# Splitting an expert's first and third weights into two buffers and two transfers, with a shorter Newton step for the norms

## The chip, the cores and the metric

The kernel runs on one core of a Trainium2 chip. The metric is the device time of one execution in microseconds. The time before is the median of three runs, 1347.77 us (1346.8 to 1350.46).

## The reference

The input is one sequence of 2048 rows of 512 numbers (float32). It is layer-normalised, and the normalised rows `xn` go two ways, whose results are added to the input:

```python
xn = layernorm(x)                       # (x - mean) / sqrt(var + 1e-5)
x + attention(xn) + ffn(xn)

# attention: 16 heads, two softmax maps each (d = 16), rotary, causal
f1, f2 = rfft(attn1, axis=time), rfft(attn2, axis=time)
f = (f1 - lambda_full * f2) * filt      # a Gaussian low-pass over time
a = irfft(f)
a = a * rsqrt(mean(a * a over the 32 of a head) + 1e-5) * rms_weight * (1 - LAMBDA_INIT)
a.reshape(T, 512) @ Wout

# ffn: 8 experts, each row goes to its best 2, and a shared expert for all rows
scores = softmax(xn @ gate_w.T); w, idx = top_k(scores, 2); w = w / sum(w)
y_e = (silu(xn @ w1[e]) * (xn @ w3[e])) @ w2[e]        # 512 -> 352 -> 512
shared = (silu(xn @ sw1) * (xn @ sw3)) @ sw2           # 512 -> 704 -> 512
```

## The kernel before

The kernel has three stages. The first normalises the rows in groups of 1, 1, 2, 4, 4 and 4 tiles of 128 rows, computes the routing, and makes rotated queries and keys, which it writes to device memory. The second, `middle`, is nine tenths of a millisecond of attention with the experts' products laid in between. The third, `ending`, does the filter over time as products with constant matrices, the norm over each head, the output product and the sum of all parts.

**Order.** In `middle` all five engines keep the order of the program text. The attention is a stream of units (one key block of one head, scores, exponential, mask, values, sums), four at a time. After each burst the loop calls `work()`, which takes the next step of the generator `experts()`. Each `yield` in that generator is one step with a weight in us, by which the loop paces the steps evenly over the stream. SyncE issues nearly all transfers, in program order: query and key loads (`qS`, `kS`) when a new attention chunk begins, the experts' weights, and the stores of the experts' rows to `ys`. Transfers share eight completion semaphores in turn, so an issue waits for the transfer eight before it.

**Experts.** Routed rows are sorted by expert into slots. A tile is 128 slots. Its steps are: `up_first`, four products `xh` with the first weights, tanh and a multiply; `up_third`, four products `xg` with the third weights and a multiply; the gather of later rows; the transpose of the next tile's rows (`xT`); and `down`, three products `xy` with the second weights, of the tile before. The first 26 tiles in `ORDER` belong to one expert each. The next six hold 64 slots of one expert and 64 of another, so that they need two sets of weights and each product is done in two halves. Two more one-expert tiles end the row. `sets[j]` says which weight sets tile `j` uses.

**Weights.** `wex` in device memory has one row of 4352 numbers per partition for each expert: first and third weights (2816, interleaved by 128-row block of the input dimension), then second weights (1536). Two more entries hold the shared expert. On chip there are two places, each with a buffer `wu` (1408 KB) and a buffer `wd` (768 KB). Set `n` uses place `n % 2`. `routed(j)` reads the expert's number on SyncE. `fetch_up` fills `wu` for set `n + 2` after `up_third` of the tile that used set `n`, since `wu` is free only then; `fetch_down` fills `wd` after `down`.

In the last block of the shared expert (steps `n` of `chunks`, in `experts`) the row order is loaded at `n == 0`, transposed at `n == 3`, and at `n == 5` the first rows are gathered and the first `fetch_up` is issued; the second follows after the block.

**Norms.** `rsqrt` and `newton` compute 1/sqrt with one Newton step: ScalarE takes the square root, VectorE the reciprocal and four more operations. VectorE adds the small constant to the variance before that (L360 in the first stage, L1237 in `means` of `Pair`, where it also divides by 32). There are six such steps in the first stage, and eight in the last, one for each pair of row tiles.

**The end.** `fetched` loads the input rows into `res`, adds the shared expert's rows, and then gathers each row's two expert rows from `ys` with adding transfers on GpSimd (L1136, L1138). `finished` and `last` add the output product on VectorE (L1289, L1300) and store.

Of the kernel before, what the change touches and what calls it, by code (L numbers as in the profile page):

```python
# [8 lines left out]
F32 = mybir.dt.float32  # L9
# [10 lines left out]
P = 128  # L20
# [30 lines left out]
WUP = NE * 2 * FI  # L51
# [18 lines left out]
def block_kernel(  # L70
# [39 lines left out]
    neglam = cpool.tile([P, 1], F32, name="neglam")  # L110
    ones = cpool.tile([P, P], F32, name="ones")
# [12 lines left out]
    def rsqrt(pool, dst, src, n):  # L124

        root = pool.tile([P, n], F32, tag="rs_root", name="rs_root")
        nc.scalar.activation(root, src, AF.Sqrt)
        newton(pool, dst, src, root, n)

    def newton(pool, dst, src, root, n):  # L130
        y = pool.tile([P, n], F32, tag="rs_y", name="rs_y")
        nc.vector.reciprocal(y, root)
        z = pool.tile([P, n], F32, tag="rs_z", name="rs_z")
        nc.vector.tensor_mul(z, src, y)
        nc.vector.tensor_mul(z, z, y)
        nc.vector.tensor_scalar(z, z, -0.5, 1.5, ALU.mult, ALU.add)
        nc.vector.tensor_mul(dst, y, z)
# [5 lines left out]
    w_sb = [  # L143
        (wp.tile([P, WUP], F32, name=f"wu{i}"), wp.tile([P, WCOL - WUP], F32, name=f"wd{i}")) for i in range(2)
    ]

    def fetch_up(e, i, eng):
        eng.dma_start(w_sb[i][0], e[:, :, :WUP].rearrange("o p w -> p (o w)"))

    def fetch_down(e, i, eng):  # L150
        eng.dma_start(w_sb[i][1], e[:, :, WUP:].rearrange("o p w -> p (o w)"))

# [4 lines left out]
    def expert(mp, fps, yp=None, stores=2, by_scalar=False):  # L157
# [19 lines left out]
        def up_half(ws, xT, i, name):  # L177
            dst = bank([P, FI], name)
            for c in range(NE):
                o = (2 * c + i) * FI  # L180
                for r, w in parts_of(ws):
                    nc.tensor.matmul(  # L182
                        dst[r, :], xT[:, c, r], w[:, o : o + FI], start=(c == 0), stop=(c == NE - 1),
                        skip_group_check=True,
                    )
            return dst

        def up_first(w, xT):

            h = up_half(w, xT, 0, "xh")  # L190
            s = mp.tile([P, FI], F32, tag="s", name="xtanh")
            nc.scalar.activation(s, h, AF.Tanh, scale=0.5)
            nc.vector.scalar_tensor_tensor(s, s, 1.0, h, ALU.add, ALU.mult)
            return s

        def up_third(w, xT, s):

            g = up_half(w, xT, 1, "xg")
            nc.vector.tensor_mul(s, g, s)
            return s  # L200

        def up(w, xT):
            return up_third(w, xT, up_first(w, xT))
# [31 lines left out]
        return up_first, up_third, up, turned_back, (down, down_products, stored), transposed  # L235

    def shared_expert(mp, fps, places=SCH):
# [4 lines left out]
        def hidden(k, x, dst=None):  # L242

            if dst is None:
                dst = fps.tile([P, x.shape[2]], F32, tag="f", name="wh")
            for c in range(NE):
                o = (NE * k + c) * P
                nc.tensor.matmul(  # L248
                    dst, w_sb[o // WUP][0][:, o % WUP : o % WUP + P], x[:, c, :], start=(c == 0), stop=(c == NE - 1)
                )  # L250
            return dst
# [29 lines left out]
        def result(us, t, which=range(SCH), y=None):  # L281

            if y is None:
                y = fps.tile([P, E], F32, tag="f", name="wy")
            for i in which:
                nc.tensor.matmul(  # L286
                    y, us[i][:, t * P : (t + 1) * P], w_sb[i // NF][1][:, i % NF * E : (i % NF + 1) * E],
                    start=(i == 0), stop=(i == SCH - 1),
                )
            return y  # L290
# [4 lines left out]
    with ExitStack() as pools:  # L295
# [38 lines left out]
        for i in range(2):  # L334
            fetch_up(wex[NX + i : NX + i + 1], i, nc.sync)
            fetch_down(wex[NX + i : NX + i + 1], i, nc.sync)
# [21 lines left out]
        def normalised(done, many, mv):  # L358
            var = lp.tile([P, many], F32, tag="var", name="var")
            nc.vector.tensor_scalar(var, mv[:, :, 1], EPS, None, ALU.add)  # L360
            rstd = lp.tile([P, many], F32, tag="rstd", name="rstd")
            rsqrt(lp, rstd, var, many)
# [158 lines left out]
        _, _, _, _, (_, _, stored), _ = expert(ep, eps, stores=EARLY)  # L521
# [76 lines left out]
    def middle(general):  # L598


        with ExitStack() as pools:
# [29 lines left out]
            def experts():  # L631
# [5 lines left out]
                _, _, _, _, (_, _, stored), _ = expert(sp, fps, mp, by_scalar=True)  # L637
                _, _, _, chunks, result = shared_expert(sp, fps)
                for t0 in range(EARLY, NT - 1, TQ):
# [3 lines left out]
                    for n, us in enumerate(chunks(xnT[:, :, cols], u_last)):  # L643
# [7 lines left out]
                        elif last and n == 3:  # L651
                            ps = bank([P, 2, NR], "ps_w")
# [4 lines left out]
                        elif last and n == 5:  # L657


                            xr = [rows_of(j) for j in ORDER[:2]]  # L660
                            es = [routed(2 * ORDER[0])]
                            fetch_up(es[0], 0, nc.sync)
                        yield 3.45 * (t1 - t0) / TQ
                    if last:
                        es.append(routed(2 * ORDER[1]))
                        fetch_up(es[1], 1, nc.sync)
# [7 lines left out]
                up_first, up_third, _, turned_back, (down, _, _), transposed = expert(rp, fps, mp, by_scalar=True)  # L674
                for i in range(2):
                    fetch_down(es[i], i, nc.sync)
# [12 lines left out]
                def tile_down(j, uT):  # L689
                    tj = ORDER[j]  # L690
                    return places(j, 1), uT, ys[tj * P : (tj + 1) * P, :], wcol[:, tj : tj + 1]

                for j in range(NR):
# [3 lines left out]
                    yield 2.9 if late else 2.4  # L697
                    u = up_third(places(j, 0), xT, half)
                    if j + 2 < NR:
                        xr.append(rows_of(ORDER[j + 2]))  # L700
                    for n in sets[j]:
# [3 lines left out]
                        fetch_up(es[n + 2], n % 2, nc.sync)  # L705
# [3 lines left out]
                    if late:  # L709
                        down(*late)  # L710
                        for n in sets[j - 1]:
                            fetch_down(es[n + 2], n % 2, nc.sync)
# [7 lines left out]
                fetch_down(wex[NX : NX + 1], 0, nc.sync)  # L720
# [381 lines left out]
    def ending():  # L1102
# [3 lines left out]
        with tc.tile_pool(name="tail1", bufs=1) as t1, tc.tile_pool(name="tail2", bufs=2) as t2, tc.tile_pool(  # L1106
# [9 lines left out]
            _, _, _, _, (_, _, stored), _ = expert(tp, fps, by_scalar=True)  # L1116
            hidden, gated, times, _, result = shared_expert(t2, fps, 2)
            fetch_down(wex[NX + 1 : NX + 2], 1, nc.scalar)
# [106 lines left out]
            class Pair:  # L1225
# [8 lines left out]
                def means(self):  # L1234
                    self.ms = tp.tile([P, 32], F32, tag="ms", name="ms")
                    nc.vector.tensor_reduce(self.ms, self.sq.rearrange("p i (h d) -> p (i h) d", d=32), AX.X, ALU.add)
                    nc.vector.tensor_scalar(self.ms, self.ms, 1.0 / 32, EPS, ALU.mult, ALU.add)  # L1237

                    self.root = tp.tile([P, 32], F32, tag="root", name="root")
                    nc.scalar.activation(self.root, self.ms, AF.Sqrt)  # L1240

                def scales(self):

                    r = tp.tile([P, 32], F32, tag="rms", name="rms")
                    newton(tp, r, self.ms, self.root, 32)
# [103 lines left out]
    with tc.If(nc.values_load(more[0:1, 0:1], min_val=0, max_val=1) > 0):  # L1349

        with tc.tile_pool(name="before_more", bufs=1) as gap, tc.tile_pool(name="more", bufs=2) as mp, tc.tile_pool(
# [3 lines left out]
            _, _, up, turned_back, (down, _, _), transposed = expert(mp, fps)  # L1355
            for j in range(NR, NS):
# [14 lines left out]
                u = up([w[:, :WUP] for w in ws], transposed(x))  # L1371
                down([w[:, WUP:] for w in ws], turned_back(u), ys[j * P : (j + 1) * P, :], pairs[:, 1:])
# [50 lines left out]
def _experts(w1, w3, w2, sw1, sw3, sw2):  # L1423
# [5 lines left out]
    for e in range(NX):  # L1429
        up = a[e, :, :WUP].reshape(P, NE, 2, FI)  # L1430
        for i, w in enumerate((w1[e], w3[e])):
            up[:, :, i] = w.reshape(NE, P, FI).transpose(1, 0, 2)
# [51 lines left out]
```

## Time and profile before

| | |
|---|---|
| time, median of three runs | 1347.77 us |
| the profiled execution's own time, and its span | 1349.09 us, 1347.3 us |
| granted TensorE clock, mean of the span | 0.994 |
| moved by DMA | 215.06 MB, mean 160 GB/s |
| weight loads `wu`, on SyncE | 44 of 1408 KB |
| weight loads `wd`, on SyncE | 44 of 768 KB (one more on ScalarE) |
| first stage and shared rows, to the first scores | 0 to about 254 us |
| attention with the shared expert's products | about 254 to 600 us |
| attention with one-expert tiles | about 600 to 1070 us |
| attention with two-expert tiles | about 1070 to 1197 us |
| last two tiles, then the third stage | about 1197 us to the end |

How to read the profile: the page gives each engine's busy time and share of the span, and in forty slices the busy tenths and the clock that TensorE was granted. A timeline row gives start, duration, engine, line of the kernel, operation, result and operands, how many instructions were merged into the row, and in brackets the idle time before it with what ended it. `PE` is TensorE, `DVE` VectorE, `ACT` ScalarE, `POOL` GpSimd, and `SPq` SyncE's queue of transfers. A row of the table of windows gives the stretch, its length, the busy time and the number of instructions of PE, PEld (weight loads into the array), DVE, ACT and POOL, then the granted clock, the busy share of the DMA engines, and GB/s. A row of waits gives who waited for what, the sum in us, how often, and the longest.

### The profile page before, as it was taken

The page shows a single profiled execution, that of the slowest core. Times are in us where ns is not written, and L with a number is a line of the kernel's source. Part 1 is how long each engine was busy: PE and PEld are TensorE (multiplying, and loading weights), DVE is VectorE, ACT ScalarE, POOL GpSimd, SP SyncE. Part 2 cuts the span into 40 slices and gives each one's busy share as a digit, 9 for nine tenths or more (in the row PEclk, how much of TensorE's full clock was granted, in tenths as well). Part 3 has the DMA queues.
Part 4 walks back from the last instruction along what each step waited for, and adds up shares of the span by engine and source line. Part 5 has one row for each costly group of instructions (what it writes and reads, how often), then busy time and mean ns, then how long its engine had stood idle before and what let it go on. Part 6 is the DMA issues. An engine that isn't in the chain of part 4 may idle for free.

```text
span 1347.3 us, 20781 instructions
## 1 busy us (share of the span) xinstructions
PE 1310.0 (97%) x7554; PEld 599.2 (44%) x7554; DVE 1014.1 (75%) x1343; ACT 689.5 (51%) x848; POOL 612.7 (45%) x639
## 2 busy tenths in 40 slices
PE   7999999999999999999999999999999989999997
PEld 3444444334343444445445444444544433345544
DVE  7049883277777769878988988888798769776885
ACT  2311110265666566676667666666676657561321
POOL 0002330012131223216986975975598457431774
PEclk9999999999999999999999999999999989999999
DMA  9405763200210122236656657565655657778997
GB/s 375 175 16 169 201 195 102 88 12 32 71 56 25 33 76 87 74 120 173 178 172 177 194 183 209 168 198 178 188 192 188 209 167 264 269 280 318 181 225 167
DMA packets 75721, 215.06 MB, mean 160 GB/s; under 512 B 12260, under 2 KB 12712, under 8 KB 69720
## 3 DMA queue, kind: packets, MB, share of 16 engines
q1 hardware_dynamic: 62888, 186.47, 42.4%
q0 software_dynamic: 11056, 22.78, 8.7%
q10 hardware_dynamic: 1664, 4.38, 1.0%
q8 instruction: 63, 1.03, 0.4%
q14 instruction: 50, 0.41, 0.1%
HBM read 170.48 MB, written 43.10 MB: 159 GB/s over the span
## 4 chain that ended last, share of the span: by engine, by line
PE 60%; POOL 9%; DMA 7%; issue 2%; DVE 2%; ACT 0%; SPq 0%; POOLq 0%; DVEq 0%; ACTq 0%
PE ps_o L875 16%; PE ps_s L831 11%; PE wh L248 8%; PE xy L218 5%; PE xh L182 5%; PE xg L182 5%; PE wy L286 4%; DMA wu<-in_wex_dram 3%; POOL res L1138 3%; DMA res<-ysh 2%; PE ps_sum L901 1%; POOL pt L853 1%; DVE sum L892 1%; PE ps_x L167 1%; PE ps_ot L913 1%
## 5 line engine op out<-in xcount | busy, mean ns | idle before, releaser
L892 DVE TENSOR_TENSOR sum<-sum,pt 128x1024 f32<-128x1024 f32 (+2 forms) x576 | 629.5, 1142 | 30.5 <-POOL pt L853 13.6
L844 ACT ACTIVATE pt<-ps_s 128x1024 f32<-128x1024 f32 x544 | 527.3, 1023 | 182.3 <-PE ps_s L831 125.3
L853 POOL TENSOR_SCALAR_AFFINE_SELECT pt<-pt 128x256 f32<-128x256 f32 (+1 forms) x224 | 163.2, 750 | 388.0 <-ACT pt L844 362.5
L875 PE MATMUL ps_o<-pt,vd 128*32 128x512 f32 (+3 forms) x2560 | 267.7, 534 | 1.9 <-POOL pt L853 1.9
L831 PE MATMUL ps_s<-qS,kS 64*128 64x512 f32 (+3 forms) x1280 | 204.6, 407 | 2.0 <-DVEq L1349 1.6
L831 PEld LDWEIGHTS ps_s<-qS,kS 64*128 64x128 f32 x1280 | 97.7, 185 | 177.9 <-issue 98.4
L248 PE MATMUL wh<-xnT,wu 128*128 128x512 f32 (+1 forms) x352 | 152.1, 580 | 0.0
L875 PEld LDWEIGHTS ps_o<-pt,vd 128*32 128x32 f32 x2560 | 67.2, 109 | 123.1 <-issue 105.7
L547 PE MATMUL ps_x<-xnT,wqk_sb 128*128 128x512 f32 x256 | 110.5, 593 | 0.0
L500 POOL DMA_INDIRECT who<-pairs,slot x32 | 34.6, 1081 | 163.1 <-DVE pairs L497 104.0
L182 PE MATMUL xh<-wu,xT 128*128 128x352 f32 (+1 forms) x320 | 93.7, 480 | 8.6 <-DMA wu<-in_wex_dram 7.8
L248 PEld LDWEIGHTS wh<-xnT,wu 128*128 128x128 f32 x352 | 64.7, 191 | 73.7 <-issue 57.8
L218 PE MATMUL xy<-wd,uT 128*128 128x512 f32 (+3 forms) x240 | 94.6, 599 | 0.8 <-DVE rcp L916 0.8
L182 PE MATMUL xg<-wu,xT 128*128 128x352 f32 (+1 forms) x320 | 88.6, 468 | 0.0
L930 POOL TENSOR_TENSOR vd<-o_n 128x128 f32<-128x128 f32 x60 | 59.0, 1002 | 53.8 <-DVE o_n L921 53.7
L547 PEld LDWEIGHTS ps_x<-xnT,wqk_sb 128*128 128x128 f32 x256 | 48.4, 190 | 60.6 <-issue 60.6
L286 PE MATMUL wy<-wd,ws 128*128 128x512 f32 x160 | 74.9, 603 | 0.0
L1138 POOL DMA_INDIRECT res<-ys,slot x32 | 54.7, 1711 | 25.5 <-DMA res<-ysh 13.5
L182 PEld LDWEIGHTS xh<-wu,xT 128*128 128x128 f32 (+1 forms) x320 | 48.4, 178 | 38.9 <-DMA wu<-in_wex_dram 8.2
L564 ACT CAST hi<-turned 128x1024 fp32r<-128x1024 f32 x16 | 16.8, 1047 | 93.8 <-DVE turned L562 59.4
L182 PEld LDWEIGHTS xg<-wu,xT 128*128 128x128 f32 (+1 forms) x320 | 46.6, 174 | 34.3 <-issue 14.8
L382 PE MATMUL ps_tv<-wv_sb,xnT 128*128 128x512 f32 x128 | 59.3, 616 | 0.7 <-ACT xnT L379 0.7
(254 smaller groups left out, 1363.1 us busy)
## 6 DMA issues: line engine op xcount, KB each, us to landing
wu<-in_wex_dram SPq DMA_DIRECT2D x44, 1408.0 KB
wd<-in_wex_dram SPq DMA_DIRECT2D x44, 768.0 KB
kS<-parts_k SPq DMA_DIRECT2D x128, 128.0 KB
qS<-parts_q SPq DMA_DIRECT2D x256, 64.0 KB
ys<-y_sb SPq DMA_DIRECT2D x34, 256.0 KB
parts_q<-hi SPq DMA_DIRECT2D x32, 256.0 KB
parts_k<-hi SPq DMA_DIRECT2D x16, 256.0 KB
parts_k<-turned SPq DMA_DIRECT2D x16, 256.0 KB
```

The source lines that it names most:

```text
L182: nc.tensor.matmul(dst[r, :], xT[:, c, r], w[:, o : o + FI], start=(c == 0), stop=(c == NE - 1), skip_group_check=True,)
L218: nc.tensor.matmul(y[r, :], uT[:m, ic, r], w[:m, ic * E : (ic + 1) * E], start=(ic == 0), stop=(ic == NF - 1), skip_group_check=True,)
L248: nc.tensor.matmul(dst, w_sb[o // WUP][0][:, o % WUP : o % WUP + P], x[:, c, :], start=(c == 0), stop=(c == NE - 1))
L286: nc.tensor.matmul(y, us[i][:, t * P : (t + 1) * P], w_sb[i // NF][1][:, i % NF * E : (i % NF + 1) * E], start=(i == 0), stop=(i == SCH - 1),)
L382: nc.tensor.matmul(pv, xnT[:, c, t * P : (t + 1) * P], wv_sb[:, c, :], start=(c == 0), stop=(c == NE - 1))
L547: nc.tensor.matmul(ps[:, i, :], wqk_sb[st, qk][:, i, c, :], xnT[:, c, cols], start=(c == 0), stop=(c == NE - 1),)
L831: nc.tensor.matmul(to, k, queries[2 * g + h, qc][r, off : off + w], start=True, stop=not general)
L844: nc.scalar.activation(pt[:, :, used], ps[:, :, used], AF.Exp, scale=SCALE)
L853: nc.gpsimd.affine_select(out=part, in_=part, pattern=[[0, part.shape[1]], [1, P]], compare_op=ALU.is_ge, fill=0.0, base=0, channel_multip ...
L875: nc.tensor.matmul(self.o[r : r + 32, off:], vd[:, kb, v0 : v0 + 32], pt[:, s, :], start=first, stop=self.ended, skip_group_check=True,)
L892: nc.vector.tensor_add(to, to, pt)
L1138: nc.gpsimd.indirect_dma_start(out=came[k], out_offset=None, in_=ys, in_offset=bass.IndirectOffsetOnAxis(ap=slot[:, step - 2, order[k] : o ...
```

## The change

The buffer for first and third weights becomes two, `w_sb[i][0]` and `w_sb[i][1]`, and second weights are `w_sb[i][2]`. The layout in device memory follows: first weights whole, then third weights whole. One function `fetch(e, i, k)` loads part `k`. In the loop over tiles the first weights of the next set are fetched after `up_first`, and the third weights at the place where both were fetched before. In the last shared block the first loads are spread over steps 3, 5 and 9 and the end of the block. The Newton step takes the small constant and the scale into fused operations, and ScalarE's square root applies both by its own scale and bias (a constant tile `tiny`), so that VectorE no longer writes the shifted variance.

```diff
-    def rsqrt(pool, dst, src, n):
-        root = pool.tile([P, n], F32, tag="rs_root", name="rs_root")
-        nc.scalar.activation(root, src, AF.Sqrt)
-        newton(pool, dst, src, root, n)
-
-    def newton(pool, dst, src, root, n):
+    def root_of(pool, src, n, by, name):
+        root = pool.tile([P, n], F32, tag=name, name=name)
+        nc.scalar.activation(root, src, AF.Sqrt, scale=by, bias=tiny)
+        return root
+
+    def newton(pool, dst, src, root, n, by):
         y = pool.tile([P, n], F32, tag="rs_y", name="rs_y")
         nc.vector.reciprocal(y, root)
         z = pool.tile([P, n], F32, tag="rs_z", name="rs_z")
-        nc.vector.tensor_mul(z, src, y)
-        nc.vector.tensor_mul(z, z, y)
-        nc.vector.tensor_scalar(z, z, -0.5, 1.5, ALU.mult, ALU.add)
-        nc.vector.tensor_mul(dst, y, z)
+        nc.vector.scalar_tensor_tensor(z, src, EPS / by, y, ALU.add, ALU.mult)
+        nc.vector.scalar_tensor_tensor(z, z, -0.5 * by, y, ALU.mult, ALU.mult)
+        nc.vector.scalar_tensor_tensor(dst, z, 1.5, y, ALU.add, ALU.mult)
...
-    def fetch_up(e, i, eng):
-        eng.dma_start(w_sb[i][0], e[:, :, :WUP].rearrange("o p w -> p (o w)"))
-
-    def fetch_down(e, i, eng):
-        eng.dma_start(w_sb[i][1], e[:, :, WUP:].rearrange("o p w -> p (o w)"))
+    spans = ((0, WONE), (WONE, WUP), (WUP, WCOL))
+    w_sb = [[wp.tile([P, b - a], F32, name=f"w{k}_{i}") for k, (a, b) in enumerate(spans)] for i in range(2)]
+
+    def fetch(e, i, k, eng=nc.sync):
+        a, b = spans[k]
+        eng.dma_start(w_sb[i][k], e[:, :, a:b].rearrange("o p w -> p (o w)"))
...
                         elif last and n == 3:
+                            es = [routed(2 * ORDER[0])]
+                            fetch(es[0], 0, 0)
...
                         elif last and n == 5:
                             xr = [rows_of(j) for j in ORDER[:2]]
-                            es = [routed(2 * ORDER[0])]
-                            fetch_up(es[0], 0, nc.sync)
+                            fetch(es[0], 0, 1)
+                        elif last and n == 9:
+                            es.append(routed(2 * ORDER[1]))
+                            fetch(es[1], 1, 0)
                         yield 3.45 * (t1 - t0) / TQ
                     if last:
-                        es.append(routed(2 * ORDER[1]))
-                        fetch_up(es[1], 1, nc.sync)
+                        fetch(es[1], 1, 1)
...
                     half = up_first(places(j, 0), xT)
+                    for n in sets[j]:
+                        m = n + 2 - len(halves)
+                        es.append(routed(halves[n + 2]) if m < 0 else wex[NX + m : NX + m + 1])
+                        fetch(es[n + 2], n % 2, 0)
                     yield 2.9 if late else 2.4
-                    u = up_third(places(j, 0), xT, half)
+                    u = up_third(places(j, 1), xT, half)
                     if j + 2 < NR:
                         xr.append(rows_of(ORDER[j + 2]))
                     for n in sets[j]:
-                        m = n + 2 - len(halves)
-                        es.append(routed(halves[n + 2]) if m < 0 else wex[NX + m : NX + m + 1])
-                        fetch_up(es[n + 2], n % 2, nc.sync)
+                        fetch(es[n + 2], n % 2, 1)
                     yield 2.4
...
-            var = lp.tile([P, many], F32, tag="var", name="var")
-            nc.vector.tensor_scalar(var, mv[:, :, 1], EPS, None, ALU.add)
             rstd = lp.tile([P, many], F32, tag="rstd", name="rstd")
-            rsqrt(lp, rstd, var, many)
+            newton(lp, rstd, mv[:, :, 1], root_of(lp, mv[:, :, 1], many, 1.0, "rs_root"), many, 1.0)
...
-                    nc.vector.tensor_scalar(self.ms, self.ms, 1.0 / 32, EPS, ALU.mult, ALU.add)
-
-                    self.root = tp.tile([P, 32], F32, tag="root", name="root")
-                    nc.scalar.activation(self.root, self.ms, AF.Sqrt)
+                    self.root = root_of(tp, self.ms, 32, 1.0 / 32, "root")
```

## The prediction

> **What bounds the kernel now.** I read the page's busy shares first, then the stages in a table of windows, then the waits of TensorE, then its timeline in the one stage where it stands still, then SyncE's queue there, and last the end of the program.
>
> ```profile
> PE 1310.0 (97%) x7554; PEld 599.2 (44%) x7554; DVE 1014.1 (75%) x1343; ACT 689.5 (51%) x848; POOL 612.7 (45%) x639
> PEclk9999999999999999999999999999999989999999
> ```
> ```profile
> 618.00:1060.00 442.00, 439.09 (x3019) 209.78 (x3018) 381.12 (x441) 295.81 (x357) 339.25 (x343) 1.00 0.60 185
> 1060.00:1197.00 137.00, 129.20 (x1007) 54.50 (x1005) 102.61 (x122) 81.33 (x100) 68.99 (x83) 0.96 0.72 244
> ```
> TensorE is busy for 97% of the span, so only its idle and its slow stretches can be won. While each 128-row tile belongs to one expert (618 to 1060) it idles 2.9 us of 442. In the stretch where six tiles each need two experts' weights (1060 to 1197) it idles 7.8 us of 137, and its mean clock is 0.96. The waits name the cause:
> ```profile
> PE xh L182 <- DMA wu<-in_wex_dram: 7.8, 4, 3.1
> PE ps_tr L1276 <- DVE a L1247: 5.4, 5, 1.7
> ```
> The first is the whole idle time of that stretch: the first product of a tile, xh, waits for `wu`, which holds first and third weights together. TensorE's timeline around it, from four windows:
> ```profile
> 1074.85 1.40 PE L182 MATMUL xh<-wu,xT 128*64 128x352 f32 x8 [1.49 <-DMA wu<-in_wex_dram]
> ...
> 1099.71 1.40 PE L182 MATMUL xh<-wu,xT 128*64 128x352 f32 x2 [3.06 <-DMA wu<-in_wex_dram]
> 1102.94 4.96 PE L182 MATMUL xh<-wu,xT 128*64 128x352 f32 x14 [1.83 <-DMA wu<-in_wex_dram]
> 1107.83 1.16 PE L831 MATMUL ps_s<-qS,kS 64*128 64x512 f32 x4
> ...
> 1124.17 3.28 PE L182 MATMUL xh<-wu,xT 128*64 128x352 f32 x16
> ...
> 1162.90 2.58 PE L182 MATMUL xh<-wu,xT 128*64 128x352 f32 x14 [1.40 <-DMA wu<-in_wex_dram]
> ```
> Fourteen products take 2.58 us at 1162.90, but 4.96 after the long wait. The windows of 4 us show why (ninth figure the granted clock, the last two the DMA share and GB/s):
> ```profile
> 1096.00:1100.00 4.00, 0.94 (x7) 0.69 (x6) 3.50 (x5) 1.45 (x2) 2.17 (x2) 0.82 0.48 123
> 1100.00:1104.00 4.00, 2.17 (x6) 0.53 (x6) 0.74 (x3) 0.00 (x0) 3.82 (x4) 0.50 0.40 121
> 1104.00:1108.00 4.00, 4.00 (x14) 1.35 (x12) 0.00 (x0) 0.07 (x1) 0.22 (x1) 0.50 0.85 269
> ...
> 1116.00:1120.00 4.00, 4.00 (x32) 1.78 (x24) 4.00 (x4) 2.85 (x4) 2.72 (x4) 1.00 0.94 391
> ```
> The clock is halved, and the DMA engines are not full while TensorE waits: issue time matters here as much as bandwidth. SyncE's queue:
> ```profile
> 1083.21 3.09 SPq L148 DMA_DIRECT2D wu<-in_wex_dram  x2
> 1086.34 16.87 SPq L745 DMA_DIRECT2D qS<-parts_q  x8
> ```
> The pair of `wu` is issued at 1083.21, when xg (the last reader of the same buffers) has just ended, and xh of the next tile wants it at 1096.7. It has landed by 1102.9.
>
> At the end two chains finish almost together:
> ```profile
> 1337.71 3.62 PE L1298 MATMUL po<-wo_sb,aT 128*128 128x256 f32 x16
> ...
> 1339.16 0.69 DVE L1289 TENSOR_TENSOR res<-res,po 128x512 f32<-128x512 f32 x1 [4.42 <-DMA res<-ys,slot]
> 1341.75 0.75 DVE L1300 TENSOR_TENSOR res<-res,po 128x256 f32<-128x256 f32 x2 [1.91 <-DMA res<-ys,slot]
> ...
> 1336.91 1.55 POOL L1138 DMA_INDIRECT res<-ys,slot  x1 [2.67 <-DMA res<-ys,slot]
> ```
> TensorE ends at 1341.3, but VectorE waits for the last gathered rows until 1341.7: GpSimd's row of gathers ends last.
>
> **The change part by part.** TensorE's and GpSimd's instructions keep kind and order. SyncE issues one transfer more for each of the 44 up loads; ScalarE's list keeps its length, with one early root a copy sooner; VectorE loses two operations per norm step.
>
> *Weights in the two-expert stretch.* First weights are now refetched when up_first of the tile has ended, third weights at the old place, after up_third. What goes if no xh waits: idle 1.49 + 3.06 + 1.83 + 1.40 = 7.78. After the long wait: 14 products 4.89 from start to the next start instead of 2.51 (2.38), the four scores behind them 1.09 instead of 0.67 (0.42), the two products between the waits 1.40 instead of 0.81 (0.59). Two xh without a named wait are stretched too: 1124.17 to 1127.38 is 3.21, and the one at 1143.01 3.31, where an undisturbed one (1181.73 to 1184.25) is 2.52: 0.69 + 0.79. Sum 12.65.
>
> Is each transfer early enough then? For the worst tile SyncE is busy with query and key loads until 1080.04 (the last key load: 1077.85 + 2.19). First weights, two sets of 704 KB, can go from there: 1.44 MB at the 250 GB/s of the disturbed windows is 6 us, so they land near 1088, and xh wants them at 1096.7, or 1093 with the earlier wait gone: 5 us to spare. Third weights go about 1081 and are wanted at about 1100 (xh 2.5, then scores, values and scores, 3.2, after 1093); even at the pace seen (19.7 us from 1083.21 to 1102.9) they land at about 1100.7. So up to 1 us may stay, and I leave 1.0 in: 11.65. The bounds are 12.65 and, if SyncE holds the first weights back so that only half the data is saved, about 6. VectorE (102.6 of 137) and ScalarE (81.3) still fit in 125 us: 82% and 65%, as in the one-expert stage (86% and 67%), where TensorE did not wait.
>
> *What the new issues cost.* An issue is 0.33 us (the rows of `wu` and `wd` on SyncE), 44 more make 15 us of a queue that mostly waits: no cost while it waits. In the program each transfer of SyncE waits for the one eight before it; that is why the query loads at 1086.34 take 16.87 us: the last two stand behind the `wu` pair. With more transfers in the ring, query loads may be later. The tight places are the shortest attention chunks: last key load issued 842.02 + 2.38 = 844.40, the next chunk begins at 846.16, 1.8 us later; at 727.21, 964.44 and 1080.04 there are 2.8, 3.7 and 6.3 us. In the instruction list of the changed program no new first-weight load stands directly before these four; directly before two of them stood a whole `wu`, now 704 KB of third weights. So I cost it at nothing, between a loss of 2 us (each of the four 3 us later: 1.2 + 0.2 lost, and the start of the products) and a gain of 1. Stores of ys and the down loads stay behind the same instructions. First weights now stand before some query loads and wait for up_first, which TensorE's order has ahead of those chunks anyway.
>
> A rule of the Trainium skill speaks against splitting: DMA: Bandwidth & Descriptors, section on the anatomy of one DMA, fits a GpSimd-issued DMA as 2.0 us fixed plus bytes by 436 GB/s. Were that paid one after another, a two-expert tile would need 4 x (2.0 + 1.65) + 2 x (2.0 + 1.8) = 22.2 us of transfers, against 20.9 per tile now (xh of the first at 1072.6 to that of the first one-expert tile at 1198.2, by six). The row decides: at 1116 to 1120, with several transfers in flight, 391 GB/s moved at a DMA share of 0.94. The fixed part overlaps; I add nothing.
>
> *Clock.* The page TensorE: Matmul & The Clock Gate (Part 1) has the half rate come after an idle window of about 3.4 us. Here the gap was 3.06, and a mean of 0.82 over 1096 to 1100 puts the drop at about 1098.6, 2 us into it. By the rule a gap of 3.06 costs only itself, and 3.4 of the 12.65 would be absent; the trace has them, so I count them.
>
> *Other moved loads.* In the last shared block the first expert's loads go two and more steps earlier. The first xh (601.9) waits for no weights today: nothing, hidden by the wh products. At the start six weight loads replace four, two issues and ring places ahead of the lambda loads; their reader ends at 39.3, and ScalarE takes it up at 45.5: 6 us of cover.
>
> *Norm step.* Six VectorE operations become four, the added ones fused. Fused and plain cost the same at equal size (L193 0.515, L199 0.517 us), so I take 0.19 each; were they as slow as the reciprocal (0.35) nothing would be won. Per pair at the end: 0.23 (L1237) + 0.19 + two gaps of 0.035 = 0.49, times 8 is 3.9 us of VectorE; TensorE's waits for `a` (5.4) may shrink by 2 to 3. But GpSimd's gathers end last, and none of their inputs is that late: 0, with 0 to 1 as bounds. Before the first tile: 0.15 + 0.16 + gaps, 0.38, ahead of TensorE's first instruction at 7.32, and TensorE is dense after it: I take 0.35. ScalarE's root with scale and bias: as before.
>
> Sum: 11.65 + 0.35 = 12.0. The tail moves along, since its first link is the store of the last expert tile (1231.88). The profiled execution took 1349.09 (span 1347.3 and 1.8 around it), so 1337.1 for it; it is 1.3 above the median of 1347.77, which gives 1335.8.
>
> **The rivals.**
> (1) SyncE holds first weights back behind query loads, so the long wait shrinks but stays: gain about 6, 1342. For: 16.87 us of blocked queue. Against: the 5 us to spare.
> (2) The end is bound by VectorE and the norm step counts: 2 more, 1333 to 1334. Against: VectorE idles 4.42 and 1.91 for gathers.
> (3) Slower: transfers pay their fixed part in turn, 22.2 us per two-expert tile, 6 x 1.3 = 8 us more: about 1356. It decides once a tile's six weight transfers take over 20.9 us. Against: the DMA share of 0.2 to 0.5 in several windows of the stretch.
> (4) Nothing: the slow landing (123 GB/s) follows the transfers wherever they are put, and third weights wait instead: within 4 us, about 1345.
>
> **How the numbers follow.** Main case 0.68, 1334 to 1338; (2) 0.08; (1) 0.13; (4) 0.06; (3) 0.05. A measurement of this kernel tells about 0.3%, 4.0 us, from no change. Main, (2) and nearly all of (1) lie beyond it: faster 0.88; same 0.07; slower 0.05. Range 1332 to 1342: (2) is its lower end, most of (1) its upper.
>
> **What would show it.** In the profile after: TensorE's wait for weights under 1.5 us in all; the granted clock at 1.00 through the two-expert stretch; that stretch about 12 us shorter; the end still on GpSimd's gathers, TensorE finishing 2 us and more before them. Wrong if xg waits for third weights, if scores wait for qS, or if the end does not move with the last store of ys.

## The result, and the profile after

The changed kernel takes 1336.14 us (median of 5 runs, 1331.87 to 1339.29) against 1347.77 for the kernel before (5 runs on the same chip): a ratio of 0.9907, 95% interval 0.9878 to 0.9936. The forecast of 1335.8 is met almost to the microsecond, but not by its own sum: one term came to two thirds of its size, and two gains that had been left at nothing made it up. The profiled execution's span is 1334.3 us, 13.0 less than before. Busy shares and clock, from the page after:

```profile
PE 1305.5 (98%) x7554; PEld 598.5 (45%) x7554; DVE 1007.7 (76%) x1316; ACT 690.5 (52%) x848; POOL 620.3 (46%) x639
PEclk9999999999999999999999999999999999999999
```

VectorE has 27 instructions fewer, TensorE the same 7554. The two stages, as windows (after the seven busy times and counts: granted clock, DMA share, GB/s):

```profile
618.00:1060.00 442.00, 438.76 (x3020) 209.40 (x3016) 381.58 (x441) 295.62 (x358) 338.59 (x341) 1.00 0.62 185
1060.00:1197.00 137.00, 133.79 (x1052) 58.60 (x1052) 109.34 (x132) 87.35 (x106) 78.87 (x83) 0.98 0.77 259
```

The second line is to be read against the promise of a clock of 1.00 and next to no idle time: 3.2 us of idle are left in it, and the clock is 0.98. TensorE's waits after:

```profile
PE xh L181 <- DMA w<-in_wex_dram: 3.2, 2, 2.1
PE ps_tr L1273 <- DVE a L1244: 2.4, 4, 1.2
```

Four waits for weights became two, and the waits for `a` fell from 5.4 to 2.4 us. Both remaining weight waits stand at the worst tile of before. TensorE's timeline, every line of xh from the first two-expert tile on and the scores behind the slow one:

```profile
1070.54 2.99 PE L181 MATMUL xh<-w,xT 128*64 128x352 f32 x16
...
1094.84 0.78 PE L181 MATMUL xh<-w,xT 128*64 128x352 f32 x2 [2.08 <-DMA w<-in_wex_dram]
1096.69 4.96 PE L181 MATMUL xh<-w,xT 128*64 128x352 f32 x14 [1.07 <-DMA w<-in_wex_dram]
1101.57 1.22 PE L831 MATMUL ps_s<-qS,kS 64*128 64x512 f32 x4
...
1117.98 2.59 PE L181 MATMUL xh<-w,xT 128*64 128x352 f32 x16
1136.11 2.59 PE L181 MATMUL xh<-w,xT 128*64 128x352 f32 x16
1153.01 2.59 PE L181 MATMUL xh<-w,xT 128*64 128x352 f32 x16
1171.83 2.59 PE L181 MATMUL xh<-w,xT 128*64 128x352 f32 x16
```

Five of the six tiles now run xh in one piece. The one at 1094.84 waits as before, only shorter, and its fourteen products take 4.96 us again, at half clock. SyncE's queue there:

```profile
1079.99 3.89 SPq L151 DMA_DIRECT2D w<-in_wex_dram  x4
1083.92 16.72 SPq L745 DMA_DIRECT2D qS<-parts_q  x8
```

The first weights were issued when the prediction said (1079.99, forecast 1080.04). They were to land near 1088. The products that wait for them start at 1094.84 and 1096.69, about 15 us after the issue of 1.44 MB.

To place all of the 13.0 us, TensorE's instructions, which come in the same order in both kernels, were laid side by side, and the lead of the changed kernel read at the stage borders:

| stretch of TensorE's list (times of before) | lead gained, us | the prediction's term |
|---|---|---|
| start to 250 | 0.1 | 0.35 |
| the branch near 254 | 1.9 | none |
| one-expert tiles, to 1066 | 0.0 | 0 |
| two-expert stretch, to the last ys store (1232) | 7.9 | 11.65 |
| tail, to TensorE's end | 2.9 | 0 |

The last rows of the program in the changed kernel, from the timelines of TensorE, VectorE and GpSimd:

```profile
1324.95 3.62 PE L1295 MATMUL po<-wo_sb,aT 128*128 128x256 f32 x16
...
1328.90 0.75 DVE L1297 TENSOR_TENSOR res<-res,po 128x256 f32<-128x256 f32 x2 [3.06 <-DMA res<-ys,slot]
...
1323.68 1.55 POOL L1138 DMA_INDIRECT res<-ys,slot  x1 [2.76 <-DMA res<-ys,slot]
```

TensorE ends at 1328.57 and the last adds start at 1328.90: still a tie, not the lead of 2 us and more that was forecast. So the gathers came earlier too. The experiments below ask whether the norm step or chance did that.

And the branch near 254, the program's `tc.If` ahead of `middle` (L1349 before, L1346 after), at which TensorE waits for VectorE's queue. TensorE before, then after:

```profile
254.45 0.84 PE L831 MATMUL ps_s<-qS,kS 64*128 64x512 f32 x4 [1.58 <-DVEq L1349]
255.22 4.97 PE L248 MATMUL wh<-xnT,wu 128*128 128x512 f32 x7
```
```profile
254.02 0.94 PE L831 MATMUL ps_s<-qS,kS 64*128 64x512 f32 x4 [1.24 <-DVEq L1346]
254.89 3.70 PE L244 MATMUL wh<-xnT,w 128*128 128x512 f32 x8
```

Seven products took 4.97 us, now eight take 3.70. The windows of before and of after, from 256 to 260, have the clock at 0.64 and 1.00:

```profile
256.00:260.00 4.00, 4.00 (x7) 1.71 (x6) 0.00 (x0) 1.94 (x2) 0.00 (x0) 0.64 0.33 108
```
```profile
256.00:260.00 4.00, 4.00 (x13) 1.59 (x12) 0.69 (x1) 3.31 (x4) 0.00 (x0) 1.00 0.41 121
```

The idle time itself is 0.34 us shorter; the other 1.6 us are a clock drop that is absent.

### The profile page after: what moved, and what is told of

The parts are those of the page before. It is cut to its first block, busy times and chain, and to the rows that moved or that the text cites. A ratio compares the mean times of both kernels' runs of the same rounds, so it can differ in the third digit from the quotient of the medians.

```text
span 1334.3 us, 20914 instructions
## 1 busy us (share of the span) xinstructions
PE 1305.5 (98%) x7554; PEld 598.5 (45%) x7554; DVE 1007.7 (76%) x1316; ACT 690.5 (52%) x848; POOL 620.3 (46%) x639
## 4 chain that ended last, share of the span: by engine, by line
PE 64%; POOL 8%; DMA 5%; issue 2%; DVE 2%; ACT 0%; SPq 0%; POOLq 0%; DVEq 0%; ACTq 0%
PE ps_o L875 17%; PE ps_s L831 12%; PE wh L244 8%; PE xy L214 6%; PE xh L181 5%; PE xg L181 5%; PE wy L283 4%; POOL res L1138 3%; DMA res<-ysh 2%; PE ps_sum L901 2%; DMA w<-in_wex_dram 1%; PE ps_x L167 1%; POOL pt L853 1%; DVE sum L892 1%; PE ps_ot L913 1%
## 5 line engine op out<-in xcount | busy, mean ns | idle before, releaser
L244 PE MATMUL wh<-xnT,w 128*128 128x512 f32 (+1 forms) x352 | 150.4, 574 | 0.0
L244 PEld LDWEIGHTS wh<-xnT,w 128*128 128x128 f32 x352 | 64.1, 190 | 72.6 <-issue 56.5
L214 PE MATMUL xy<-w,uT 128*128 128x512 f32 (+3 forms) x240 | 94.6, 599 | 1.2 <-DVE rcp L916 1.2
L181 PE MATMUL xh<-w,xT 128*128 128x352 f32 (+1 forms) x320 | 90.4, 477 | 4.0 <-DMA w<-in_wex_dram 3.2
L181 PE MATMUL xg<-w,xT 128*128 128x352 f32 (+1 forms) x320 | 88.6, 468 | 0.0
L283 PE MATMUL wy<-w,ws 128*128 128x512 f32 x160 | 74.8, 603 | 0.0
L181 PEld LDWEIGHTS xh<-w,xT 128*128 128x128 f32 (+1 forms) x320 | 48.3, 178 | 31.0 <-issue 9.3
L181 PEld LDWEIGHTS xg<-w,xT 128*128 128x128 f32 (+1 forms) x320 | 46.6, 174 | 34.4 <-issue 14.8
```

What stands on the lines that cost most here:

```text
L181: nc.tensor.matmul(dst[r, :], xT[:, c, r], w[:, c * FI : (c + 1) * FI], start=(c == 0), stop=(c == NE - 1), skip_group_check=True,)
L214: nc.tensor.matmul(y[r, :], uT[:m, ic, r], w[:m, ic * E : (ic + 1) * E], start=(ic == 0), stop=(ic == NF - 1), skip_group_check=True,)
L244: nc.tensor.matmul(dst, w_sb[o // WUP][o % WUP // WONE][:, o % WONE : o % WONE + P], x[:, c, :], start=(c == 0), stop=(c == NE - 1),)
L283: nc.tensor.matmul(y, us[i][:, t * P : (t + 1) * P], w_sb[i // NF][2][:, i % NF * E : (i % NF + 1) * E], start=(i == 0), stop=(i == SCH - 1),)
```

## The experiments

**What holds the weights back.** The packet records of the trace gave the lead: from 1076 to 1083, behind the four key loads issued at 1076.22, packets of 2 KB pass at a steady 24 in each microsecond, 84 ns each. That is the work of two engines. The windows of the changed kernel say the same:

```profile
1077.00:1078.00 1.00, 1.00 (x10) 0.49 (x8) 1.00 (x2) 1.00 (x2) 0.83 (x2) 1.00 0.15 49
1078.00:1079.00 1.00, 1.00 (x10) 0.37 (x6) 0.86 (x2) 0.58 (x1) 1.00 (x2) 1.00 0.13 49
```

A DMA share of 0.13 is 2 of 16 engines, and 49 GB/s is 24 packets of 2 KB per us. A key load fills 64 partitions from 32 rows, read twice by a broadcast whose outermost dimension is two. Four of them are 256 packets. On two engines that is 128 each, and 10.8 us by an estimate from the 84 ns of a packet. The Trainium skill has the rule for it (DMA: Bandwidth & Descriptors, "Why a DMA increments its semaphore by 16 and not by 1"): a transfer runs on the largest number of engines, up to 16, that divides the slowest dimension of both sides, and on SyncE's queue on the lowest-numbered ones. By that rule all key loads share the same two engines, and a weight transfer, which spreads over sixteen, is whole only when its share on those two is through. The experiment `keys_32` writes each key load as two loads of 32 rows, and `before_keys_32` does it to the kernel before:

```diff
-                        nc.sync.dma_start(
-                            k[64 * s : 64 * s + 64, :].bitcast(F32),
-                            src.unsqueeze(0).to_broadcast([2, 2 * D, QC]),
-                        )
+                        for rep in range(2):
+                            r = 64 * s + 32 * rep
+                            nc.sync.dma_start(k[r : r + 32, :].bitcast(F32), src)
```

> The changed kernel with each key load of 64 rows (32 rows read twice by a broadcast) written as two loads of 32 rows. Theory C (a key load with the broadcast outermost runs on two of the 16 DMA engines only, 24 packets of 2 KB per us from 1076 to 1083, and weights issued behind it wait for these two engines): the four first and third weights of tile 27 land within 6 us of their issue, TensorE's wait of 3.2 us and the half clock after it are gone, the two-expert stretch is 4 to 6 us shorter: 1330 to 1332. Theory D (the landing is set by the bytes that are asked for at once): the weights land as late, 1336. Theory E (SyncE's ring of eight transfers is what delays): the extra issues make it worse, 1337 to 1340, with waits for qS or kS.

> The kernel before with the key loads as two loads of 32 rows each, the weights unsplit. Theory C: the pair issued at 1083.21 lands by about 1092 instead of 1102.9, so the wait of 3.06 and 1.83 us and the half clock go: about 7 us, 1340 to 1341, most of what the split gave. Theory D: 1347 to 1348.

Measured, on one chip, where the kernel before took 1348.68: `keys_32` 1330.93 (1330.54 to 1332.16), ratio 0.9869 (0.985 to 0.9888); `before_keys_32` 1338.40, ratio 0.9928 (0.991 to 0.9945). Respelling the key loads alone is worth 10 us, more than the forecast of 7; in its profile the two-expert stretch alone gained 11.1. In `keys_32` SyncE's queue, TensorE's xh of the worst tile, and the stretch:

```profile
1080.09 2.76 SPq L151 DMA_DIRECT2D w<-in_wex_dram  x4
1082.90 9.98 SPq L744 DMA_DIRECT2D qS<-parts_q  x8
```
```profile
1092.16 2.59 PE L181 MATMUL xh<-w,xT 128*64 128x352 f32 x16
```
```profile
1060.00:1197.00 137.00, 136.14 (x1092) 59.11 (x1084) 114.93 (x138) 91.87 (x112) 92.87 (x90) 1.00 0.76 260
```

The weights leave at the same time as in the changed kernel, and xh starts without a wait; no wait for weights is left in TensorE's list. It is close, though, and not the landing within 6 us that was expected: the last packets of the weights pass at 1091, about 11 us after the first issue. The bytes of the window 1084 to 1088 tell the two apart, first the changed kernel, then `keys_32`:

```profile
1084.00:1088.00 4.00, 4.00 (x19) 2.04 (x17) 3.41 (x6) 2.37 (x4) 3.74 (x7) 1.00 0.99 303
```
```profile
1084.00:1088.00 4.00, 4.00 (x17) 1.57 (x19) 3.93 (x7) 2.37 (x5) 3.76 (x5) 1.00 1.00 397
```

The share is full in both, and 303 GB/s against 397 pass. In the changed kernel's packet records the weights then trickle from 1094 to 1098 at 8 or 9 packets of 5.6 KB in each microsecond, 216 to 254 ns each: two engines again, with the others through. The 250 GB/s that the prediction had taken for a pace of all engines was a mean over unlike ones. Theory D (bytes) and E (SyncE's ring) fall; the extra issues cost nothing.

Is it the dimension of two, or that the same rows are read twice? `keys_two_blocks` reads two different blocks of 32 rows, with the same bytes, packets and shape:

```diff
-                        src = parts[1][2 * h + s, :, :, c * QC : (c + 1) * QC].rearrange("a d t -> (a d) t")
-                        nc.sync.dma_start(
-                            k[64 * s : 64 * s + 64, :].bitcast(F32),
-                            src.unsqueeze(0).to_broadcast([2, 2 * D, QC]),
-                        )
+                        o = min(2 * h + s, 2 * NH - 3)
+                        src = parts[1][o : o + 3 : 2, :, :, c * QC : (c + 1) * QC].rearrange("b a d t -> b (a d) t")
+                        nc.sync.dma_start(k[64 * s : 64 * s + 64, :].bitcast(F32), src)
```

> The changed kernel with each key load reading two different blocks of 32 rows (one of its own, one two places on) instead of the same 32 rows twice: the keys are wrong in half of their rows, so the attention is, but bytes, packets and transfers are the same. Theory C1 (the outermost dimension of two decides on how many DMA engines a transfer runs): 24 packets of 2 KB per us again behind a key load, weights of tile 27 land as late, 1335 to 1338. Theory C2 (reading the same rows twice is what is slow): the key loads go as fast as in keys_32, 1330 to 1332.

1336.35 (1335.06 to 1337.39), beside 1336.91 for the changed kernel on the same chip (`after_again`, below). One window behind its key loads, and its wait for weights:

```profile
1077.00:1079.00 2.00, 2.00 (x16) 0.74 (x12) 1.53 (x3) 0.80 (x1) 1.99 (x3) 1.00 0.20 50
```
```profile
PE xh L181 <- DMA w<-in_wex_dram: 3.6, 2, 3.0
```

50 GB/s again, and the wait is there. The outermost dimension decides, not the rereading.

**Does the earlier place of the first weights matter?** `split_late` keeps the split, and asks for first weights where the pair was asked for before:

```diff
                     half = up_first(places(j, 0), xT)
-                    for n in sets[j]:
-                        m = n + 2 - len(halves)
-                        es.append(routed(halves[n + 2]) if m < 0 else wex[NX + m : NX + m + 1])
-                        fetch(es[n + 2], n % 2, 0)
                     yield 2.9 if late else 2.4
                     u = up_third(places(j, 1), xT, half)
...
+                    for n in sets[j]:
+                        m = n + 2 - len(halves)
+                        es.append(routed(halves[n + 2]) if m < 0 else wex[NX + m : NX + m + 1])
+                        fetch(es[n + 2], n % 2, 0)
                     for n in sets[j]:
                         fetch(es[n + 2], n % 2, 1)
```

> The changed kernel with the first weights of the next set asked for at the old place (after up_third), first weights of the set ahead of its third weights. Theory C (the landing at tile 27 is set by the two DMA engines that still work off key loads; issue times matter little): within 2 us of the changed kernel, whose run stands beside this one. Theory F (the gain comes from asking earlier): the gain of the stretch falls to under half, 1340 to 1342.

1336.57 (1335.59 to 1337.02) against 1336.91: the same, theory F falls. At the worst tile the weights leave at 1080.92 instead of 1079.43 and xh waits 4.1 us instead of 2.8. (Its list of waits puts 3.6 of them down to VectorE, whose `sum` was what ended last by the profile.) The place at which first weights are asked for moves their issue by only 1.5 us here, since in both kernels they stand behind the same query and key loads. So the split's gain does not come from asking earlier; by elimination it comes from xh needing half of the data, which no run tests alone.

**What the norm step is worth.** `split_only` is the changed kernel with the old step, `norm_only` the kernel before with the new one (the diff is shown in part; the rest of the old step comes back with it):

```diff
-            nc.vector.scalar_tensor_tensor(z, src, EPS / by, y, ALU.add, ALU.mult)
-            nc.vector.scalar_tensor_tensor(z, z, -0.5 * by, y, ALU.mult, ALU.mult)
-            nc.vector.scalar_tensor_tensor(dst, z, 1.5, y, ALU.add, ALU.mult)
+            nc.vector.tensor_mul(z, src, y)
+            nc.vector.tensor_mul(z, z, y)
+            nc.vector.tensor_scalar(z, z, -0.5, 1.5, ALU.mult, ALU.add)
+            nc.vector.tensor_mul(dst, y, z)
...
```

> The changed kernel with the old six-operation norm step. Theory A (the split gives about 8 us in the two-expert stretch, and the norm step gives about 3 at the end, by moving TensorE's chain of transposes): 1339 to 1340, and the time from the last ys store (xy) to the end is about 110 us, as before the change. Theory B (the end hangs on GpSimd's gathers alone, and the 3 us that the end lost are chance): 1336 to 1337, the end about 107 us after the last ys store.

> The kernel before with the short norm step alone. Theory A: 1344 to 1345, TensorE's waits for `a` down from 5.4 to about 2.4 us, and the gathers' end moves with them. Theory B: 1347.5 within 1 us; TensorE's waits shrink, but the last adds wait longer for the gathered rows.

On one chip (before: 1348.68): `split_only` 1340.13, ratio 0.994 (0.9923 to 0.9956); `norm_only` 1343.38, ratio 0.997 (0.9957 to 0.9982). The times fit theory A within 0.7 us and not theory B: the norm step is worth something. The two parts do not add up, however: 8.5 and 5.3 make 13.8, and both together gained 11.1 to 11.6. On top of the norm step the split is worth 6.5 to 7.2 (`norm_only` against the two medians of the changed kernel, taken on other chips). TensorE's waits for `a`, first in `split_only`, then in `norm_only`:

```profile
PE ps_tr L1276 <- DVE a L1247: 5.1, 5, 1.7
```
```profile
PE ps_tr L1273 <- DVE a L1244: 2.4, 4, 1.2
```

Was the end's tie chance? A second profile of the kernel before, of `split_only`, and runs of the changed kernel again:

> The kernel before, a second profile. If the 1.9 us at the branch near 254 and the end's tie are of the old norm step: TensorE idles about 1.6 us at the branch with a dropped clock behind it, TensorE ends 109.4 us after the last ys store and the end follows it. If they are chance: no drop in this profile, or the gathers end well after TensorE.

> The split with the old norm step, a second profile: the branch idles about 1.6 us again; in the first profile the clock held there. A drop now says that at 1.6 us it falls by chance; none, that the split has a part in it. TensorE ends 109.1 to 109.5 us after the last ys store, whatever the gathers do.

> The changed kernel itself, once more, beside the others on this chip. Chance in the landing of weights and of gathered rows: 1333 to 1339 with a spread of 4 us and more over its runs, where keys_32 had 1.6; TensorE idles about 1.25 us at the branch near 254 without a drop of the clock behind it; TensorE ends 106.5 us after the last ys store, and the gathers' last issue falls between 100.7 and 105 us after it.

`before_again` took 1353.5, `split_only_b` 1340.36 (one run each), `after_again` 1336.91 (1335.81 to 1337.16). The spread of 4 us and more that was expected of `after_again` did not come: its six runs lie within 1.4. The end of `before_again`, TensorE, VectorE, GpSimd:

```profile
1342.73 3.62 PE L1298 MATMUL po<-wo_sb,aT 128*128 128x256 f32 x16
...
1344.66 0.42 DVE L1300 TENSOR_TENSOR res<-res,po 128x256 f32<-128x256 f32 x1 [1.04 <-PE po L1298]
1346.38 0.42 DVE L1300 TENSOR_TENSOR res<-res,po 128x256 f32<-128x256 f32 x1 [1.30 <-PE po L1298]
...
1337.81 1.54 POOL L1138 DMA_INDIRECT res<-ys,slot  x1 [1.36 <-DMA res<-ys,slot]
```

Here the last adds wait for TensorE, not for gathered rows. Measured from the last store of ys, in us:

| kernel | TensorE ends after | last gather is issued after | program ends after |
|---|---|---|---|
| before, before_again, before_keys_32 (old step) | 109.45, 109.44, 109.49 | 105.03, 100.90, 103.43 | 115.46, 114.84, 115.05 |
| split_only, split_only_b (old step) | 109.14, 109.14 | 100.74, 102.95 | 114.52, 114.77 |
| after, after_again, split_late, norm_only (new step) | 106.55, 106.75, 107.13, 106.57 | 101.67, 103.06, 102.78, 101.31 | 112.33, 114.12, 113.08, 111.86 |
| five more with the new step, named in this section | 106.49 to 107.62 | 102.05 to 103.59 | 112.22 to 114.17 |

TensorE's end stays within 0.4 us with the old step and 1.1 with the new one; GpSimd's gathers wander over 4 us with the old one. The profile that the prediction was read from has the latest gathers of all. TensorE was the lasting bound. Shortened by 1.5 to 3.0 us, it hands the end to the gathers: in all nine profiles of the new step the last adds wait for gathered rows, in `norm_only` at no cost, in `after_again` so long that 1.4 us of TensorE's lead are lost. So the 2.9 us of the first pair are TensorE's own lead. At the program's end the new step is worth 1.9 us by the means of five and nine profiles (114.9 and 113.0).

The same kernels tell of the branch near 254. With the old step TensorE idles 1.58 to 1.68 us there, and in four of five profiles (before, before_again, before_keys_32, split_only_b) the clock drops behind it; in `split_only` it didn't. With the new step the gap is 1.2 to 1.4 us, and none of nine profiles has a drop. So the profile of `norm_only` holds 2.0 us from the branch and 2.9 from the tail, and its median gained 5.3. Why the gap is 0.35 us shorter is not settled: no norm step stands near it in VectorE's timeline. It goes with the step in all fourteen profiles, and that is all that is shown. The profile of `norm_only` has a span 9.7 us shorter, since 4.4 us more came in the two-expert stretch with weights as before (5.3 us of waits instead of 7.8); `before_again` has 1.9 there. So much does the landing vary by itself, and the 7.9 us of the result, read from one pair of profiles, have that uncertainty; the medians give the split 8.5 alone and 6.5 to 7.2 beside the norm step.

**What is the split worth where key loads are spread?** `norm_keys_32` is the kernel before with the new norm step and the key loads of 32 rows; its difference to `keys_32` is the split.

> The kernel before with the short norm step and with key loads of 32 rows, the weights unsplit: what is the split still worth once the key loads are spread? By the kernels before_keys_32 (1338.4) less what the norm step gave alone (5.3, of which about 3 at the end): 1333 to 1335.5; the split is then worth 2 to 4 us on top of it, as xh waits a little for wu (0.8 us in before_keys_32) and the start is the same. If the split is worth its whole 8 us beside spread key loads: 1338 to 1339.

> The kernel norm_keys_32 again, beside keys_32: 1333 to 1335 if the split is worth 2 to 3 us, else 1331.

> The kernel keys_32 again, beside norm_keys_32 on one chip: 1330 to 1332. If the split is worth 2 to 3 us beside spread key loads (the two-expert stretch gained 13.5 in keys_32 and 10.9 in norm_keys_32), this one is that much faster; if those were chance, the two are equal.

First 1333.92 (ratio 0.9891, 0.9867 to 0.9916), on another chip than `keys_32`. Then both on one chip: 1333.62 for `norm_keys_32_b` (1332.89 to 1335.71) and 1330.74 for `keys_32_b` (1329.44 to 1331.89), whose ratio to the kernel before is 0.9875 (0.9858 to 0.9892). The split is worth 2.9 us there. The two-expert stretch gained 13.4 us in both profiles of `keys_32` and 10.8 to 10.9 in those of `norm_keys_32`. `keys_32` is faster than both kernels of this case, by 17.4 to 17.8 us against the kernel before.

## Why the prediction came out right, step by step

*The bound.* Right: the wait of xh for weights, and the clock behind it, was where most of the time lay.

*Two-expert stretch, 11.65 of 12.65.* Mis-sized: it gave 7.9. The parts that did not hang on the landing came as counted: the first tile 1.9 (1.49 counted), the two stretched xh 0.7 and 0.8 (0.69 and 0.79), the last wait even 2.2 (1.40 counted). The step that failed is the landing: "1.44 MB at the 250 GB/s of the disturbed windows is 6 us, so they land near 1088". They took 15, the tile kept its wait and its half clock, and of its 8.28 us only 2.3 came. `keys_32` gave the rest: 13.4 in the stretch, and in the trace of `keys_32_b` the second set's first weights have landed at 1088.99. The 250 GB/s was an average over engines; what lands last is ruled by the two that still work off key loads. The low share ahead of the weights was in the profile before, and the prediction read such shares as free engines:

```profile
1080.00:1082.00 2.00, 2.00 (x18) 1.24 (x20) 2.00 (x3) 1.95 (x3) 1.83 (x3) 1.00 0.13 48
```

*Rival (1).* Its outcome (the long wait shrinks but stays) came in part, by another mechanism. SyncE did not hold first weights back; they were issued on time and queued behind keys in the engines themselves. The stretch's 7.9 lies between its 6 and the main case's 11.65, but its cause was not the one that acted.

*Norm step at the end, 0.* Wrong: 2.9 in this pair, 1.9 by the means of all profiles. The saving on VectorE and the shrinking of TensorE's waits (5.4 to 2.4) were as counted; the step that failed is "GpSimd's gathers end last". That was true of one profile by 0.4 us. Rival (2), put at 0.08 with 2 us more, was right on this term.

*The branch, not in the sum.* 1.9 us, of which 1.6 is a clock drop behind a gap of 1.58 us. The gap stood in TensorE's list of waits before, with 1.6 us. The prediction counted clock only where it followed a wait for weights, and gave no reason to leave this gap out.

*Start, 0.35.* TensorE starts 0.38 earlier, but the lead is gone at 14.6 (-0.17) and 0.1 at 250. "TensorE is dense after it" was wrong: in the profile before, its transposes `ps_tv` still wait seven times for `vd`, 2.0 us in all. Against the profile before, the lead at 250 is -1.1 to -0.1 in the four others of the old step and -0.6 to 0.7 in the nine of the new one. Such scatter neither shows 0.35 us nor rules it out.

*Moved loads and 44 more issues, 0.* Right: no xg waits for third weights, no scores wait for queries, and `split_late` shows the place of the first weights to be worth nothing either way.

*Fixed part of a DMA, paid in parallel.* Right: the 22.2 us of rival (3), an estimate from the skill's figure, would have shown in the tiles behind the worst one, which follow each other at 17 to 19 us and run xh without a wait. Rival (4) was right in part: at one tile the landing did follow the transfers, though for none of its reasons.

*Sum.* 12.0 us were forecast, and 0.1 + 1.9 + 7.9 + 2.9, with 0.2 at the last adds, came to 13.0 in this profile. That the two agree is luck: two errors of 3.75 and 4.8 us cancel.

## What to carry to other kernels

Before a landing time is estimated from GB/s, look at what the DMA engines are doing when the transfer is issued: a share of 0.13 at a steady rate is two engines with a queue, and a transfer that spreads over all sixteen lands when these two are through. Spell loads so that the outermost dimension is the rows, not a broadcast of two. Where two chains tie at the end, take a second profile before calling one of them the bound: the chain that moves between profiles is the wrong one to build on.

## What was not expected of the hardware

- A load of 64 x 2 KB with an outermost dimension of two passes at 24 packets per us on two engines; as two loads of 32 rows each it spreads. The respelling is worth 10 us of 1348 in the kernel before. Whether it also narrows the runs is open: the six of `before_keys_32` range over 5.6 us, the fourteen of the kernel before on that chip over 6.8.

- The kernel before loses time in more than one place by chance. In `before_again`, its longest profile, a score waits for queries at one of the four tight places that the prediction named (846.16), and with the clock behind it that costs 6.4 us.

```profile
846.39 1.53 PE L831 MATMUL ps_s<-qS,kS 64*128 64x512 f32 x3 [2.81 <-DMA qS<-parts_q]
848.86 0.76 PE L831 MATMUL ps_s<-qS,kS 64*128 64x512 f32 x1 [0.93 <-DMA qS<-parts_q]
```

- The clock fell behind gaps much shorter than the 3.4 us that the Trainium skill gives (TensorE: Matmul & The Clock Gate, Part 1). At the branch it fell behind 1.58 to 1.68 us in four of five profiles, and behind 1.2 to 1.4 in none of nine; a gap made 0.35 us shorter went with 1.9 us less. By a rule of 3.4 us only the 0.35 would have been won there. At the worst tile of the changed kernel it fell behind 2.08 us, so the prediction was right to count the drop from the trace. But the length of the gap alone does not decide. TensorE waits as long for `a` in the tail, 1.7 us in all five profiles of the old step, and no drop follows. Here is that wait in the kernel before, and the window with the clock at 1.00; what makes the difference is not settled.

```profile
1296.86 0.66 PE L1276 MATMUL ps_tr<-cst,a 128*128 128x128 f32 x4 [1.72 <-DVE a L1247]
```
```profile
1296.00:1300.00 4.00, 3.14 (x11) 1.71 (x12) 3.97 (x6) 0.69 (x2) 3.39 (x3) 1.00 1.07 239
```
